# Second layer's experts with a part of the list each, their sends in the cross attention's units, their second matrices loaded beside the shared network; the values in three buffers

## The chip, the cores and the metric

The kernel runs on one core of a Trainium2 chip. The metric is the device time of one execution in microseconds (us): the median of several. Before the change it is 3898.57 us, the median of 3 runs (3896.55 to 3901.43).

Engines: PE is TensorE (matrix multiplications; PEld are its weight loads), DVE is VectorE, ACT is ScalarE, POOL is GpSimd, SP is SyncE, which here only issues DMA transfers. Everything is float32.

## The reference

A decoder of two layers on x of 32 batches x 100 tokens x 256, with a context of 361 tokens x 192 for each batch. Each layer is an attention, a cross attention and a feed-forward part, each added to x. The change touches the second layer's cross attention and its feed-forward part, a mixture of experts:

```python
def _L1_xattn_ref(x, context, ln_gamma, ln_beta, Wq, Wkv, Wo, bo, mask):
    # layer norm, queries from x, keys and values from the context,
    # 16 heads of 64, softmax over the 361 context tokens, out @ Wo + bo

def _L1_ffn_ref(x, shared_w1, shared_w2, experts_w1, experts_w2, gate_w):
    x_flat = x.reshape(T, D)                       # 3200 tokens x 256
    shared = jnp.einsum('td,dh->th', x_flat, shared_w1.T)
    shared = jnp.einsum('th,hd->td', jax.nn.silu(shared), shared_w2.T)
    gate_logits = x_flat @ gate_w.T
    top_k_gates, top_k_idx = jax.lax.top_k(gate_logits, TOP_K)     # 2 of 8 experts
    top_k_gates = jax.nn.softmax(top_k_gates, axis=1)
    gates = zeros.at[jnp.arange(T)[:, None], top_k_idx].set(top_k_gates)
    h = jnp.einsum('td,ehd->teh', x_flat, experts_w1)
    expert_out = jnp.einsum('teh,edh->ted', jax.nn.silu(h), experts_w2)
    selected = jnp.einsum('ted,te->td', expert_out, gates)
    return (shared + selected).reshape(B, S, D)

x = x + _L1_xattn_ref(_layernorm(x), ctx_768, ..., mask)
x = x + _L1_ffn_ref(_layernorm(x), ...)
```

## The kernel before

One program runs the six parts one after another: the first layer to about 1556 us of the trace, the second layer's attention to 1940, its cross attention from 1944 to 3186, the shared network of its feed-forward part from 3190 to 3414, its experts from 3418 to 3875, and a copy of the result to the end at 3898.

**The order.** In the stages of interest the instructions of PE, DVE, ACT and POOL are issued in the order of the program text (`in_order()`); in the shared network and the experts it is PE, DVE, ACT and SP that are fixed, and POOL's order is found by a scheduler. Each engine works through its queue in order, so an instruction that waits holds everything behind it. PSUM tiles for intermediate results come from a few rings: `mm` (single banks), `sc` (two tiles of two banks each), `po`.

**Cross attention** (L1404 to L1690). There are 128 units n (four for each of 32 batches); 16 units make one of 8 groups of 4 batches, and `at` is n % 16. Unit n (`turn_of`) transposes the softmax weights of unit n on PE (L1563) and multiplies them with the values (`sums`, L1581); meanwhile it makes the scores of unit n+2 (`scores`, L1531, in two halves c), the keys of unit n+3, and, for a pair of units, the values: an even unit computes context rows 0 to 255 (two chunks of 128 rows x 512 columns), an odd one the last 105 rows (two halves of 256 columns). The values pass from a PSUM tile `sc` to SBUF in two copies, one on ACT (L1517) and one on DVE (L1519), into one tile `vb`; the second half of the scores needs that `sc` tile again. `divided` computes a reciprocal on DVE (L1555), by which POOL multiplies the softmax weights of the next unit (L1556, 2.59 us); the next unit's transposes wait for this.

Between these stand, by `part_of`, the pieces of work that come once in a group: `finish` of a batch (product with Wo and the addition to x), `normed` (layer norm for the queries of the next group: at=1 the statistics on DVE, L162 to L169 with a power on POOL at L170, at=2 the centering), the queries, and `gating` of the group before: at=2 statistics, 3 centering and a store to `xn_dram`, 4 eight transposes, 5 the product with the gate's weights (eight matmuls of eight columns) and the choice of the two best experts, 6 their shares. All of it stands ahead of the unit's values, keys and `divided`.

**The list of experts.** `sorted_dram` has a row for each pair of token and expert, in blocks of 128 rows of one expert, 57 blocks at most. Its rows are first filled with `empty` (57 stores at the beginning of the cross attention; they point at a spare row). In the shared network `places_of` (two matmuls of 256 columns and a chain on DVE) computes from all choices where each pair goes: experts follow each other without a gap of more than a block. `send` writes 100 rows of a batch to their places with an indirect DMA from POOL (L1845), 64 in all. `pace` (L1891) is a copy of one element of `hT` on POOL, ahead of each eight sends, so that these are spread over the stage.

**Shared network** (L1712 to L1896). 104 units (h, m): `hidden` multiplies 256 tokens with a piece of the first matrix (L207), ACT applies Silu into `hT` (L1762, four buffers), and two units later `added` multiplies with the second matrix (L1770). SP loads tokens (`xn`, L1722), the sums so far (`acc`), and one matrix of an expert (`wx1`, 1 MB) per eight units.

**Experts** (L1900 to L1995). SP loads the experts' second matrices `wx2` (8 x 1 MB) and the blocks `xg` (four ahead, six buffers); each load of a block waits for all sends. Per block: two transposes (L1923), the first product (L207, `sc<-wx,xgT`), Silu, eight transposes, the second product, and an indirect DMA that adds the rows to `acc_dram`. The number of a block's expert is loaded into a register of PE.

Of the kernel before, what the change touches and what calls it, by code (L numbers as in the profile page):

```python
# [18 lines left out]
P = 128  # L19
B, T, D = 32, 100, 256  # L20
S2, DC = 361, 192
G = 4
# [9 lines left out]
ROW = D + E + 1  # L32
BIG = 3.0e38
# [32 lines left out]
def kernel(ctx: ExitStack, tc: tile.TileContext, io: dict, out: bass.AP):  # L66
# [1284 lines left out]
    sorted_dram = dram.tile([TILES * P, ROW], F32, name="sorted_dram")  # L1351
    wg = early.tile([P, 2, E], F32, name="f1_wg")
    nc.scalar.dma_start(wg, io["f1_wg"].rearrange("(c p) n -> p c n", p=P))
    hot = early.tile([T, 2, B, E], F32, name="hot1")
    gated = {}

    def gating(pool, g, part):
# [13 lines left out]
        elif part == 3:  # L1371
# [14 lines left out]
            for k in range(2):  # L1386
                nc.gpsimd.tensor_copy(hot[:, k, own, :], hots[:T, k])
# [4 lines left out]
            gated[g] = df, hots  # L1392
        else:
            df, hots = gated.pop(g)
# [8 lines left out]
            nc.vector.tensor_tensor(gates, gates, hots[:T, 1], ALU.add)  # L1403

    with tc.tile_pool(name="x1", bufs=2) as pool, tc.tile_pool(name="x1p", bufs=1) as fixed:
# [3 lines left out]
        def context(b):  # L1409
# [8 lines left out]
        empty = fixed.tile([P, ROW], F32, name="empty")  # L1418
        nc.gpsimd.memset(empty, 0.0)
        nc.sync.dma_start(acc_dram[NTOK:, :], empty[:, :D])  # L1420
        nc.gpsimd.iota(
            empty[:, D + E : ROW].bitcast(I32), pattern=[[0, 1]], base=NTOK, channel_multiplier=1
        )
        for t in range(TILES):
            nc.sync.dma_start(sorted_dram[t * P : (t + 1) * P, :], empty)
# [61 lines left out]
        def values(u, last, part):  # L1487
# [25 lines left out]
            for e, (at, kn, c0, n) in enumerate(parts):  # L1513
                src = ps[:kn, e, :n].rearrange("p (h d) -> p h d", d=64)
                dst = vb[:kn, 2, 4 * e : 4 * e + 4, :] if last else vb[:kn, e, :, :]
                if e == 0:
                    nc.scalar.copy(dst, src)  # L1517
                else:
                    nc.vector.tensor_copy(dst, src)  # L1519
# [53 lines left out]
        def sums(u, eT, vb, oT):  # L1573

            q4 = u % 4
            po = po_tile()
            for m in range(2):
                for k, (k0, kn) in enumerate(CCH):
                    for e in range(2):
                        h = 2 * m + e  # L1580
                        nc.tensor.matmul(  # L1581
                            po[64 * e : 64 * e + 64, m * T : (m + 1) * T],
                            vb[:kn, k, 4 * (u % 2) + h, :], eT[:kn, k, h, :],
                            start=(k == 0), stop=(k == 2), tile_position=(0, 64 * e),
                        )
            nc.vector.tensor_copy(
                oT[:, 2 * q4 : 2 * q4 + 2, :].rearrange("p m t -> p (m t)"), po[:, : 2 * T]
            )
# [17 lines left out]
        def value_tile():  # L1606
            return pool.tile([P, 3, 8, 64], F32, tag="vb", name="vb")
# [8 lines left out]
        def part_of(n):  # L1616
# [4 lines left out]
            if g + 1 < NG:  # L1621
                if at in (1, 2):
                    normed(g + 1, at - 1)
# [6 lines left out]
            if n >= 18 and (n - 18) % 16 < 5:  # L1630
                gating(pool, (n - 18) // 16, (n - 18) % 16)

        def turn_of(n):
# [10 lines left out]
            if v < NU:  # L1644
                if not last:
                    vbs[v // 2] = value_tile()
                values(v, last, 0)
            if n + 3 < NU:
                keys(n + 3, 0)
            if -1 <= n and n + 1 < NU:  # L1650
                divided(n + 1)
            if v < NU:
# [9 lines left out]
            if n >= 0:  # L1662
                if n % 4 == 0:
                    oTs[n // 4] = pool.tile([P, 8, T], F32, tag="oT", name="oT", bufs=1)
                sums(n, eT, vbs[n // 2], oTs[n // 4])

# [19 lines left out]

# [12 lines left out]
    nc.gpsimd.memset(ones8, 1.0)  # L1699

    before = fixed.tile([T, 2, P], F32, name="before")
    nc.gpsimd.memset(before, 1.0)
    nc.gpsimd.affine_select(
        before[:, 0, :], before[:, 0, :], pattern=[[1, P]], compare_op=ALU.is_gt,
        fill=0.0, base=0, channel_multiplier=-1,
    )
    pos = fixed.tile([T, 2, B], U32, name="pos1")
# [3 lines left out]
    SP = mybir.EngineType.SP  # L1711
    with tc.tile_pool(name="f1s", bufs=2, side="right") as pool, in_order(SP):  # L1712
# [73 lines left out]
        def places_of():  # L1786

            hs = pool.tile([T, B, E], F32, name="hs", bufs=1)
            nc.vector.tensor_tensor(hs, hot[:, 0], hot[:, 1], ALU.add)
            flat = hs.rearrange("p c e -> p (c e)")  # L1790
            pr = mm_tile()
            nc.tensor.matmul(pr[:, : B * E], before[:, 0, :], flat, start=True, stop=True)
            pt = mm_tile()
            nc.tensor.matmul(pt[:, : B * E], before[:, 1, :], flat, start=True, stop=True)

            tot = pool.tile([P, E, B], F32, tag="tot", name="tot", bufs=1)
            nc.vector.tensor_copy(tot, pt[:, : B * E].rearrange("p (c e) -> p e c", e=E))
            go = pool.tile([P, E, B], F32, tag="go", name="go", bufs=1)
            nc.gpsimd.memset(go, 1.0)
            nc.gpsimd.memset(go[:, :, 0:1], 0.0)  # L1800
            cum = pool.tile([P, E, B], F32, tag="cum", name="cum", bufs=1)
            nc.vector.tensor_tensor_scan(
                cum.rearrange("p e c -> p (e c)"), go.rearrange("p e c -> p (e c)"),
                tot.rearrange("p e c -> p (e c)"), 0.0, ALU.mult, ALU.add,
            )

            nb = pool.tile([P, E], F32, tag="nb", name="nb", bufs=1)
            nc.vector.tensor_scalar(
                nb, cum[:, :, B - 1], 1.0 / 128, 0.49609375, ALU.mult, ALU.add
            )  # L1810
# [4 lines left out]
            beg = pool.tile([P, E], F32, tag="beg", name="beg", bufs=1)  # L1815
            nc.vector.tensor_tensor(beg, end, nb, ALU.subtract)
            nc.vector.tensor_scalar(beg, beg, 128.0, None, ALU.mult)

            nc.vector.tensor_tensor(cum, cum, tot, ALU.subtract)
            nc.vector.tensor_tensor(cum, cum, bc(beg, 2, B), ALU.add)  # L1820
            at = pool.tile([T, B, E], F32, tag="at", name="at", bufs=1)
            nc.vector.tensor_tensor(
                at, pr[:T, : B * E].rearrange("p (c e) -> p c e", e=E),
                cum[:T].rearrange("p e c -> p c e"), ALU.add,
            )
            pf = pool.tile([T, 2, B], F32, tag="pf", name="pf", bufs=1)
            for k in range(2):
                nc.vector.tensor_tensor(hs, hot[:, k], at, ALU.mult)
                nc.vector.tensor_reduce(pf[:, k, :], hs, AX.X, ALU.add)
            nc.vector.tensor_copy(pos, pf)  # L1830
# [4 lines left out]
            nc.vector.tensor_reduce(ef, le, AX.X, ALU.add)  # L1835
            nc.vector.tensor_scalar(ef, ef, float(E - 1), None, ALU.min)
# [3 lines left out]
            )  # L1840

        def send(b):

            for k in range(2):
                put = nc.gpsimd.indirect_dma_start(  # L1845
                    sorted_dram[:, :],
                    bass.IndirectOffsetOnAxis(ap=pos[:, k, b : b + 1], axis=0),
                    xrows[b // G][:, b % G, :], None,
                )

                if sent:
                    tc.keep_in_program_order(put)
                    tc.declare_no_dep(put.ins, group="sends", reason="the places of tokens differ")
                tc.add_to_no_dep_group("sends", put.ins)
                sent.append(put.ins)

        gating(pool, NG - 1, 0)
# [7 lines left out]
        for n in range(len(units) + 2):  # L1867
# [17 lines left out]
            if n in (4, 8, 12):  # L1885
                gating(pool, NG - 1, n // 4 + 1)
            if n == 14:
                places_of()
            if n >= 27 and n % 7 == 6 and n // 7 < 3 + B // 4:

                nc.gpsimd.tensor_copy(pace, hTs[units[n]][0:1, 0:1])  # L1891
                for b in range(4 * (n // 7) - 12, 4 * (n // 7) - 8):
                    send(b)
        store(NHB - 1)
    xpool_cm.__exit__(None, None, None)
    norms_cm.__exit__(None, None, None)  # L1896
    early_cm.__exit__(None, None, None)
    wx2_cm = tc.tile_pool(name="wx2", bufs=1)
    wx2_pool = wx2_cm.__enter__()
    wx2 = wx2_pool.tile([P, E, 8, D], F32, name="wx2")  # L1900
    with tc.tile_pool(name="f1t", bufs=2, side="right") as pool, in_order(SP):
        for e in range(E):
            nc.sync.dma_start(wx2[:, e], io["f1_w2"][e + 1].rearrange("(c p) n -> p c n", p=P))
        xgs, xgTs, hgTs, experts_ = {}, {}, {}, {}

        def get(t):

            xg = pool.tile([P, ROW], F32, tag="xg", name="xg", bufs=6)
            load = nc.sync.dma_start(xg, sorted_dram[t * P : (t + 1) * P, :])
            for put in sent:  # L1910
                tc.add_manual_dep(
                    load.ins, put.name,
                    mybir.DependencyInfo(
                        mybir.DependencyClass.Sync, mybir.DependencyReason.DATA
                    ),
                    reason="all rows are there",
                )
            xgs[t] = xg
# [203 lines left out]
```

## Time and profile before

| what | value |
|---|---|
| median of 3 runs | 3898.57 us |
| the profiled execution | 3899.32 us |
| its span in the trace | 3897.6 us |
| mean granted clock of TensorE | 0.964 |
| PE busy | 3581.0 us (92%) |
| PE weight loads | 2243.9 us (58%) |
| DVE busy | 1962.1 us (50%) |
| ACT busy | 1549.4 us (40%) |
| POOL busy | 1329.7 us (34%) |

The costliest groups of the stages that the change touches (line, engine, operation, output and inputs with their shapes, count; busy us in all, mean ns of one; the engine's idle time before them and what ended most of it):

```profile
L1556 POOL TENSOR_TENSOR ex<-ex,rc 100x1444 f32<-100x1444 f32 x128 | 331.9, 2593 | 492.7 <-DVE rc L1555 492.7
L1531 PE MATMUL sc<-kT,qT 64*100 64x361 f32 x1024 | 203.1, 473 | 13.0 <-DVE vb L1519 13.0
L1563 PE MATMUL mm<-ident,ex 100*128 100x100 f32 (+1 forms) x1536 | 163.6, 256 | 8.9 <-POOL ex L1556 8.2
L207 PE MATMUL sc<-wx,xgT 128*128 x456 | 206.9, 597 | 0.3 <-DMA xg<-sorted_dram 0.3
```

Idle time of an engine costs something only where that engine is the one that the others wait for. The busy PE of the page is an average over stages with different limits, so the stages are read one by one. The chain of waits that ended last holds only the last few instructions of the program here, so the stages are read from busy sums over stretches of time, from waits within a stretch, and from the timelines of single engines. The clock of PE is the share of full speed that the chip granted it.

### The profile page before, as it was taken

What the parts mean: (1) busy time and instruction counts of PE and PEld (TensorE: products, weight loads), DVE (VectorE), ACT (ScalarE), POOL (GpSimd) and SP (SyncE); (2) the same over time, 40 slices, a digit from 0 to 9 for tenths busy, and PEclk for the clock granted to TensorE, in tenths of its full rate; (3) what the DMA queues carried; (4) which work ended last, traced back from release to release, by engine and by line L of the source; (5) the groups of instructions that cost most, each with busy time, mean ns of one, the idle gap of its engine ahead of it and who ended that gap; (6) DMA issues with size and microseconds to landing.
All of it is one profiled execution on the core that took longest, in us unless ns stands there. A gap on an engine that the chain in (4) does not pass through costs nothing. (4 is left out here: it accounts for less than half of the span.)

```text
span 3897.6 us, 65045 instructions
## 1 busy us (share of the span) xinstructions
PE 3581.0 (92%) x25566; PEld 2243.9 (58%) x25566; DVE 1962.1 (50%) x5533; ACT 1549.4 (40%) x3318; POOL 1329.7 (34%) x949
## 2 busy tenths in 40 slices
PE   7888999996889899799999999999999996999998
PEld 5665565554545453333356666666666665867675
DVE  6776666654677766565544454544544531012221
ACT  4554555553222220456644444444444441212121
POOL 3344666664444532101122232332322326012111
PEclk9999999998899989899999999999999998999999
DMA  2001000000000000400100000000000014512222
GB/s 79 2 2 58 18 20 20 18 5 15 1 1 1 1 1 0 122 1 1 34 10 16 15 20 11 20 16 15 16 15 16 15 46 140 165 35 34 34 35 57
DMA packets 94185, 110.18 MB, mean 28 GB/s; under 512 B 14142, under 2 KB 87430, under 8 KB 93290
## 3 DMA queue, kind: packets, MB, share of 16 engines
q1 hardware_dynamic: 79596, 88.40, 7.9%
q0 software_dynamic: 12304, 14.28, 2.3%
q8 instruction: 204, 3.34, 0.4%
q10 hardware_dynamic: 1982, 3.35, 0.3%
q14 instruction: 99, 0.81, 0.1%
HBM read 74.02 MB, written 35.23 MB: 28 GB/s over the span
## 5 line engine op out<-in xcount | busy, mean ns | idle before, releaser
L1556 POOL TENSOR_TENSOR ex<-ex,rc 100x1444 f32<-100x1444 f32 x128 | 331.9, 2593 | 492.7 <-DVE rc L1555 492.7
L1547 ACT ACTIVATE ex<-s,nmx 100x361 f32<-100x361 f32 x512 | 303.2, 594 | 145.4 <-DVE nmx L1538 145.4
L363 POOL TENSOR_TENSOR s<-s,nmx 100x800 f32<-100x800 f32 x128 | 194.7, 1522 | 378.1 <-DVE nmx L362 359.1
L1198 ACT ACTIVATE h<-sc,cols 128x800 f32<-128x800 f32 x256 | 222.3, 924 | 135.0 <-PE sc L1192 134.7
L207 PE MATMUL mm<-f_we,x1T 128*100 128x512 f32 x512 | 267.6, 654 | 4.3 <-DVE x L1008 2.3
L1538 DVE CUSTOM_DVE_ANT_0 s<-sc,mb 100x361 f32<-100x361 f32 x512 | 250.4, 528 | 0.1
L1519 DVE COPY vb<-sc 128x512 f32<-128x512 f32 (+1 forms) x128 | 71.5, 558 | 352.5 <-ACT vb L1517 352.5
L1974 POOL DMA_INDIRECT acc_dram<-y,xg x57 | 88.2, 1547 | 420.2 <-DVE y L1973 343.3
L1531 PE MATMUL sc<-kT,qT 64*100 64x361 f32 x1024 | 203.1, 473 | 13.0 <-DVE vb L1519 13.0
L207 PE MATMUL sc<-wx,xgT 128*128 x456 | 206.9, 597 | 0.3 <-DMA xg<-sorted_dram 0.3
L207 PE MATMUL po<-wx,hgT 128*128 x912 | 206.2, 379 | 0.3 <-ACT hgT L1956 0.3
L207 PEld LDWEIGHTS po<-wx,hgT 128*128 128x128 f32 x912 | 173.2, 190 | 47.9 <-issue 26.8
L170 POOL TENSOR_TENSOR rs<-va,neghalf 100x4 f32<-100x4 f32 (+1 forms) x96 | 92.7, 969 | 306.8 <-DVE va L169 217.8
L1973 DVE TENSOR_SCALAR y<-po,gx 128x256 f32<-128x256 f32 x57 | 27.6, 484 | 331.0 <-PE po L207 331.0
L1502 PE MATMUL sc<-x_wa,cT 128*128 128x512 f32 (+1 forms) x512 | 187.7, 489 | 0.0
L1517 ACT COPY vb<-sc 128x512 f32<-128x512 f32 (+1 forms) x128 | 61.3, 479 | 316.3 <-PE sc L1507 316.3
L1021 DVE SCALAR_TENSOR_TENSOR x<-mm,wt,x 100x256 f32<-100x256 f32 x256 | 123.6, 483 | 116.1 <-PE mm L207 109.7
L375 PE MATMUL mm<-ident,ex 100*100 100x100 f32 x1024 | 126.4, 262 | 58.9 <-ACT eT L384 22.7
L1472 PE MATMUL mm<-cT,x_wa 128*128 128x361 f32 x512 | 176.3, 467 | 0.0
L1581 PEld LDWEIGHTS po<-eT,vb 128*64 128x64 f32 (+1 forms) x3072 | 136.8, 137 | 67.3 <-issue 66.9
L1563 PE MATMUL mm<-ident,ex 100*128 100x100 f32 (+1 forms) x1536 | 163.6, 256 | 8.9 <-POOL ex L1556 8.2
L384 ACT COPY eT<-mm 100x400 f32<-100x400 f32 x192 | 92.4, 493 | 193.9 <-PE mm L375 193.4
(331 smaller groups left out, 7704.0 us busy)
## 6 DMA issues: line engine op xcount, KB each, us to landing
wx<-in_f_w SPq DMA_DIRECT2D x16, 1024.0 KB
sorted_dram<-empty SPq DMA_DIRECT2D x57, 132.5 KB
xg<-sorted_dram SPq DMA_DIRECT2D x57, 132.5 KB
cb<-in_ctx SPq DMA_DIRECT2D x32, 192.0 KB
cT<-in_ctxT SPq DMA_DIRECT2D x32, 180.5 KB
cT<-in_ctxT SPq DMA_DIRECT2D x64, 90.2 KB
x<-in_x SPq DMA_DIRECT2D x8, 400.0 KB
x_dram<-x SPq DMA_DIRECT2D x32, 100.0 KB
```

The lines of the kernel that those rows point to most:

```text
L207: nc.tensor.matmul(ps, lhsT[k], rhs[k], start=(k == 0), stop=(k == n - 1))
L363: nc.gpsimd.tensor_tensor(sm, sm, bc(nmx, 2, T), ALU.add)
L375: nc.tensor.transpose(pt[:T, j * T : (j + 1) * T], exs[s, r // 2][:, 4 * (r % 2) + j, :], ident[:T, :T],)
L1198: nc.scalar.activation(h1, both[r2][:, :, :GT], AF.Tanh, bias=col("a1_b1", o))
L1472: nc.tensor.matmul(kTs[u][c][:, :S2], x1_wa[:, m * P : (m + 1) * P], cT[:, 0, :], start=True, stop=False,)
L1502: nc.tensor.matmul(ps[:kn, e, :n], cT[:, 0, at], x1_wa[:, 1024 + c0 : 1024 + c0 + n], start=True, stop=False,)
L1531: nc.tensor.matmul(ps[:T, e, :S2], qT[p0 : p0 + 64, m, tok], kT[p0 : p0 + 64, c, :], start=True, stop=True,)
L1538: nc.vector.tensor_tensor_reduce(s[:, e, :], ps[:T, e, :S2], mb, 1.0, 3.4e38, ALU.add, ALU.min, nmx[:, e : e + 1],)
L1547: nc.scalar.activation(ex[:, 2 * c + e, :], s[:, e, :], AF.Exp, bias=nmx[:, e : e + 1], scale=-1.0, accum_out=sm[:, 2 * c + e : 2 * c + e ...
L1556: nc.gpsimd.tensor_tensor(ex, ex, bc(rc, 2, S2), ALU.mult)
L1563: nc.tensor.transpose(pt[:kn, j * T : (j + 1) * T], ex[:, j, k0 : k0 + kn], ident[:T, :T])
L1581: nc.tensor.matmul(po[64 * e : 64 * e + 64, m * T : (m + 1) * T], vb[:kn, k, 4 * (u % 2) + h, :], eT[:kn, k, h, :], start=(k == 0), stop=( ...
```

## The change

1. `sorted_dram` has a region of 3328 rows (RG) for each expert, plus 128 rows. The 57 stores of `empty` fall away. In their place, behind each expert's last row, 128 empty rows are sent (`rest`, 8 indirect DMAs), and one store fills the last 128 rows.
2. `gating` keeps a running count of each expert's rows (`base`) and has a sixth part, which gives the group's places at once: three small matmuls and a few DVE operations. `places_of` becomes `blocks_of`, which only makes the list of blocks: each block's expert and first row (`rows_at`).
3. The sends of group g (8 per group) go into units 6 to 13 after unit 16g+17, behind the unit's other work; those of the last group and the rests into units 16 to 30 of the shared network, two for each pace.
4. The norms' statistics and centerings move: `norms_of` stands behind `divided` and ahead of the end of the values (`gating` parts 0 and 1 at at=1 and 2, `normed` at at=3 and 4), and the other parts of `gating` come at at=3 to 6.
5. The values lie in three tiles (`vb0`, `vb1`, `vb2`). In odd units one copy on DVE (105x512) takes the place of two.
6. The loads of `wx2` stand in the shared network (from unit 42 on, one per six units), and the first four blocks are loaded at unit 92. Each load of a block reads its first row from `rows_at` into a register of SP.
7. At the beginning of the shared network SP first stores the spare rows of `acc_dram` and the last 128 rows of `sorted_dram`; POOL makes `empty` there.

```diff
-    sorted_dram = dram.tile([TILES * P, ROW], F32, name="sorted_dram")
+    sorted_dram = dram.tile([E * RG + P, ROW], F32, name="sorted_dram")
...
+    base = w5.tile([P, E], F32, name="base1")
+    nc.vector.tensor_scalar(base, row("iota", P), float(RG), None, ALU.mult)
...
     def gating(pool, g, part):
...
+            nc.vector.tensor_tensor(hs, hots[:T, 0], hots[:T, 1], ALU.add)
+            nc.vector.memset(hc[:, 0], 0.0)
+            for i in range(G):
+                nc.vector.tensor_tensor(hc[:, i + 1], hc[:, i], hs[:, i], ALU.add)
+            nc.vector.tensor_copy(hh, hots[:T])
...
+        else:
+            df, hots, hs, hc, hh = gated.pop(g)
+            pl = mm_tile()
+            n = G * E
+            nc.tensor.matmul(
+                pl[:, :n], before[:, 0, :], hs.rearrange("p i e -> p (i e)"),
+                start=True, stop=False,
+            )
+            nc.tensor.matmul(
+                pl[:, :n], before[:, 1, :], hc[:, :G].rearrange("p i e -> p (i e)"),
+                start=False, stop=True,
+            )
+            nc.tensor.matmul(
+                pl[:, n : n + E], before[:, 1, :], hc[:, G], start=True, stop=True
+            )
...
+            nc.vector.tensor_tensor(base, base, pl[:, n : n + E], ALU.add)
...
+            for k in range(2):
+                nc.vector.tensor_tensor(hh[:, k], hh[:, k], at, ALU.mult)
+                nc.vector.tensor_reduce(pf[:, k, :], hh[:, k], AX.X, ALU.add)
+            nc.vector.tensor_copy(pos[:, :, own], pf)
...
-        for t in range(TILES):
-            nc.sync.dma_start(sorted_dram[t * P : (t + 1) * P, :], empty)
...
-            for e, (at, kn, c0, n) in enumerate(parts):
-                src = ps[:kn, e, :n].rearrange("p (h d) -> p h d", d=64)
-                dst = vb[:kn, 2, 4 * e : 4 * e + 4, :] if last else vb[:kn, e, :, :]
-                if e == 0:
-                    nc.scalar.copy(dst, src)
-                else:
-                    nc.vector.tensor_copy(dst, src)
+            if last:
+                nc.vector.tensor_copy(vb[2][:kn].rearrange("p (e n) -> p e n", e=2), ps[:kn, :, :n])
+            else:
+                nc.scalar.copy(vb[0], ps[:, 0, :])
+                nc.vector.tensor_copy(vb[1], ps[:, 1, :])
...
         def part_of(n):
...
-                if at in (1, 2):
-                    normed(g + 1, at - 1)
...
-            if n >= 18 and (n - 18) % 16 < 5:
-                gating(pool, (n - 18) // 16, (n - 18) % 16)
+            if n >= 19 and 2 <= (n - 17) % 16 < 6:
+                gating(pool, (n - 17) // 16, (n - 17) % 16)
+
+        def norms_of(n):
+            g, at = n // 16, n % 16
+            if n >= 17 and at in (1, 2):
+                gating(pool, g - 1, at - 1)
+            if g + 1 < NG and at in (3, 4):
+                normed(g + 1, at - 3)
...
             if -1 <= n and n + 1 < NU:
                 divided(n + 1)
+            if n >= 0:
+                norms_of(n)
             if v < NU:
                 values(v, last, 1)
...
+                q, m = (n - 17) // 16, (n - 17) % 16 - 6
+                if n >= 17 and 0 <= m < 8:
+                    send(q * G + m // 2, m % 2)
...
+    def get(t):
+        xg = blocks.tile([P, ROW], F32, tag="xg", name="xg", bufs=6)
+        at = nc.sync.value_load(rows_at[0:1, t : t + 1], min_val=0, max_val=E * RG)
+        load = nc.sync.dma_start(xg, sorted_dram[bass.ds(at, P), :])
...
+        nc.sync.dma_start(acc_dram[NTOK:, :], empty[:, :D])
+        nc.sync.dma_start(sorted_dram[E * RG :, :], empty)
         gating(pool, NG - 1, 0)
         rows_of(0)
...
-            if n in (4, 8, 12):
-                gating(pool, NG - 1, n // 4 + 1)
-            if n == 14:
-                places_of()
-            if n >= 27 and n % 7 == 6 and n // 7 < 3 + B // 4:
+            if n in (4, 8, 12, 14):
+                gating(pool, NG - 1, {4: 2, 8: 3, 12: 4, 14: 5}[n])
+            if n == 18:
+                blocks_of()
+            if n >= 16 and n % 2 == 0 and n < 32:
                 nc.gpsimd.tensor_copy(pace, hTs[units[n]][0:1, 0:1])
-                for b in range(4 * (n // 7) - 12, 4 * (n // 7) - 8):
-                    send(b)
+                for k in range(2):
+                    b = B - G + (n - 16) // 2
+                    if n < 24:
+                        put(send(b, k))
+                    else:
+                        e = n - 24 + k
+                        put(nc.gpsimd.indirect_dma_start(
+                            sorted_dram[:, :],
+                            bass.IndirectOffsetOnAxis(ap=rest[:, e : e + 1], axis=0), empty, None,
+                        ))
...
+            if n >= 42 and n % 6 == 0 and n // 6 < 7 + E:
+                e = n // 6 - 7
+                nc.sync.dma_start(
+                    wx2[:, e], io["f1_w2"][e + 1].rearrange("(c p) n -> p c n", p=P)
+                )
+            if n == 92:
+                for t in range(4):
+                    get(t)
```

## The prediction

> **What bounds the kernel now.** The page's slices come first: busy tenths per 97 us and the granted TensorE clock.
>
> ```profile
> PE   7888999996889899799999999999999996999998
> PEclk9999999998899989899999999999999998999999
> ```
>
> TensorE is the wall over the second half, with one dip in both rows at slice 34, the shared network of the second layer. Next the busy sums of chosen stretches (bounds, span, then busy us of PE, weight loads, DVE, ACT, POOL, then clock, DMA share, GB/s).
>
> ```profile
> 2500.00:2700.00 200.00, 197.31 (x1379) 124.80 (x1377) 89.42 (x315) 93.30 (x259) 57.50 (x30) 1.00 0.05 15
> 3200.00:3300.00 100.00, 69.18 (x334) 60.06 (x332) 15.51 (x52) 17.14 (x40) 55.27 (x58) 0.86 0.43 133
> 3600.00:3700.00 100.00, 100.00 (x433) 71.03 (x432) 21.54 (x62) 20.35 (x25) 18.54 (x12) 1.00 0.21 34
> 3380.00:3390.00 10.00, 10.00 (x49) 8.79 (x48) 0.69 (x1) 2.19 (x6) 0.00 (x0) 1.00 1.09 354
> ```
>
> Cross attention (first row) and experts (third) run PE at 99 and 100%; the shared network (second) at 69%, with POOL busy for 55. Who holds PE there is told by the waits between 3130 and 3520 us (total, times, longest), then by PE's own timeline (start, length).
>
> ```profile
> PE sc L1770 <- ACT hT L1762: 34.3, 2, 19.7
> ACT hT L1762 <- POOL pace L1891: 42.8, 2, 23.9
> ```
>
> ```profile
> 3274.99 2.07 PE L1770 MATMUL sc<-w,hT 128*128 128x256 f32 x4 [19.68 <-ACT hT L1762]
> 3278.34 1.03 PE L1770 MATMUL sc<-w,hT 128*128 128x256 f32 x4
> 3303.50 2.07 PE L1770 MATMUL sc<-w,hT 128*128 128x256 f32 x4 [14.64 <-ACT hT L1762]
> 3308.78 1.05 PE L207 MATMUL mm<-xT,w 128*128 128x256 f32 x4
> ```
>
> POOL issues 64 sends (0.99 us, 0.30 between two) from 3228.74 on. The pace copy stands behind them and reads one of four hT buffers; ACT can't refill it, PE starves twice, and four matmuls take 2.07 us instead of 1.03 afterwards.
>
> **The change, part by part.** *Shared network.* In the changed program 8 sends and 8 rest sends stand there, two per two units, the first from the unit at which the places of the last group are ready (some 5 us for the four sends ahead of the first pace). A unit takes 1.73 us, so a pace comes 3.46 us after the last, while two sends need 2×1.29 = 2.58: POOL keeps up, and a buffer of four is read in time. Removed: 19.68 + 14.64 = 34.3 of stall, and the slow matmuls after them: 3274.99 to 3278.34 is 3.35 us for work of 1.73 (+1.6); 3303.50 to 3308.78 is 5.28 for 2.59 (+2.7). The two 256-column matmuls of places_of (0.9) go, three small ones (0.5) come. Sum −38.9. Were one pace late by a pair of sends at each of a few places, some 9 us would stay: range −30 to −39.
>
> *End of the shared network.* The loads of wx2 and of the first four blocks move ahead of its last units.
>
> ```profile
> 3189.96 1.94 PE L1735 MATMUL mm<-ident,xn 128*128 128x128 f32 x8 [4.10 <-DMA xn<-xn_dram]
> 3418.76 0.66 PE L1923 MATMUL mm<-ident,xg 128*128 128x128 f32 x2 [4.95 <-issue]
> 3421.44 5.37 PE L207 MATMUL sc<-wx,xgT 128*128 x8 [0.26 <-DMA xg<-sorted_dram]
> 3428.90 3.60 PE L207 MATMUL sc<-wx,xgT 128*128 x8
> ```
>
> PE's 4.95 us of idle (3413.8 to 3418.76) go; of the slow matmuls (5.37 against 3.60) I take 2.0 in all with the 0.66 against 0.38 before it. That is −7; but the first expert matmul then also waits for the last acc stores, which land at about 3416.7, so −6.5. Range −4 (only most of the idle) to −8.5 (with the 1.08 us between the two transposes). The eight loads of wx2 stand on SP's queue between loads of xn, acc and wx1. One stretch of eight units (13.8 us) then has about 3.1 MB to move, 224 GB/s; the fourth row of the stretches shows 354 GB/s with PE busy for all of its 10 us: 0. If they queued as long as PE waits above for one xn load (4.10) at each of two turns: +8.
>
> *Junction.* In the changed order SP issues the acc_dram tail, the last x_dram row store and the sorted_dram tail ahead of the first xn load, and the second of them waits for a POOL addition that now stands behind nine small setup operations, the zeroing of the 132.5 KB tile `empty` among them. Before, xn was issued at 3186.00 and the x_dram store at 3187.85; with two issues of 0.3 to 0.4 it comes at about 3188.7. The wait of 4.10 grows by that: +2.7 (range 2 to 5).
>
> *Cross attention.* 128 units; its waits (1970 to 3180 us), and one odd unit and the start of the next on PE and DVE:
>
> ```profile
> DVE vb L1519 <- ACT vb L1517: 348.2, 126, 6.7
> PE sc L1531 <- DVE vb L1519: 12.8, 64, 0.4
> PE mm L1563 <- POOL ex L1556: 8.2, 10, 3.2
> ```
>
> ```profile
> 3062.93 0.68 PE L1507 MATMUL sc<-x_wbv,cT 64*105 64x256 f32 x4
> 3064.66 0.77 PE L1531 MATMUL sc<-kT,qT 64*100 64x361 f32 x4
> 3062.71 0.18 DVE L1555 RECIPROCAL rc<-sm 100x4 f32<-100x4 f32 x1 [1.55 <-ACT ex L1547]
> 3064.07 0.42 DVE L1519 COPY vb<-sc 105x256 f32<-105x256 f32 x1 [1.18 <-ACT vb L1517]
> 3067.99 0.42 DVE L162 BATCH_NORM_STATS2 st<-x 100x6 f32<-100x256 f32 x1
> 3070.24 0.17 DVE L169 TENSOR_SCALAR va<-mv 100x4 f32<-100x4 f32 x1
> ```
>
> The second half of the scores (PE at 3064.66) needs the PSUM tile that DVE's copy of the values (3064.07) empties. The statistics of a norm (3067.99 to 3070.32: 2.33 us) stood ahead of the reciprocal, where they delayed only POOL's ex multiply. Now they stand behind it and ahead of that copy. At at=1 of a group: reciprocal done 3062.8, statistics to 3065.13, a copy now whole on DVE (0.69, the length of a 128x512 one) to 3065.82, scores at 3065.88 instead of 3064.66: +1.22, seven times +8.5. At at=3 the eight transposes of gating, now in that same unit, lengthen PE by 0.69 and hide that much: +0.53, seven times +3.7. At at=4 seven more small DVE operations and a centering (1.38) stand there: between 0 and 0.85 each, I take 0.25: +1.7. Waits of PE for ex that the new place avoids: 8.2 less the longest and three more at the ends of the stage that stay (3.2, 0.2, 0.6, 0.6) = −3.6. The running counts add three matmuls per group, at 0.18 (eight small ones take 1.43 at 3096.32): +3.7. Sum +14; without the collisions 0, with all at their upper ends +18.
>
> The three buffers for the values are meant to free DVE's copy from ACT's (348.2 us of waits, though PE loses only 12.8 of them). In the built program that copy still waits for ACT's, since both read one PSUM tile: 0. Were it gone, an even unit would lose its excess over an odd one (0.98 against 0.61 from keys to the second scores, 0.78 against 0.71 behind them): 64×0.45 = −29. The 64 ACT copies of 0.37 that go are no gain: ACT is busy 47%.
>
> 56 sends come onto POOL behind the ex multiply (2.59) of units at=7 to 14. POOL idles 4.49 to 6.97 ahead of the next multiply, and a send takes 1.29 with its issue: 0. If a send grew past that idle time, every microsecond beyond would cost 56. [...]
>
> *Costed at nothing.* The 57 stores of `empty` (132.5 KB each) ran at 1581 to 1619 us where SP had nothing else to do. Each block load gets a register load on SP and an address from it: a block takes some 8 us and SP does only this; the nearest row is PE's own register load, at most the 1.08 us between two transposes. Upper end +17, 0.3 per block (the 0.26 at 3421.44 that PE waits for a block's rows).
>
> **Sum.** −38.9 − 6.5 + 2.7 + 14 = −29 (−28.7). The profiled execution took 3899.3 us (span 3897.6), 0.75 above the median 3898.57: 3870.6 against the one, 3869.9 against the other. I say 3870. Its own range, from the terms' ends, is 3862 to 3879.
>
> **Rivals.**
> - *The statistics don't collide.* If DVE's and PE's slack absorbs them, cross attention stays even: 3870 − 14 = 3856. For it: the waits for ex vanish and DVE is busy under half. Against: PE is at 99%, so nothing there is slack.
> - *Part of the stall stays.* POOL's rest sends hold a pace (9, by the bound above) and the wx2 loads an xn load (8); hardly both whole, so I take 14 of the 17: 3884. For it: the same pace copy still reads hT behind sends. Against: 2.58 us of sends per 3.46.
> - *The values' wait goes after all*: 3870 − 29 = 3841. Against: the wait is in the program.
> - *The block loads become the bound* (slower). SP must read a row number into a register before each of 57 loads, in order. Two blocks' first matmuls lie 7.98 us apart (3428.90 and 3436.88); from there on the experts would follow SP, and at 9 us each they cost 57×1.02 = 58 more: 3870 + 58 = 3928. For it: nothing else on SP is so serial. Against: an issue of 0.39 and a register load of 1.08 at most make 1.5 us of work per 7.98.
> - *The change doesn't do what it says*: as to the third buffer that is already my forecast; as to the sends it would need the paces to come late, which is the second rival.
>
> **How the numbers follow.** Forecast 0.58, no collision 0.14, part of the stall 0.14, values' wait 0.04, slower rival 0.06, gains and losses that cancel 0.04. The range takes the forecast and the two neighbours with their own spread, 3853 to 3887; outside lie the last three and tails, under 0.2. What a measurement here can tell from no change is 0.2%, 7.8 us. Faster (below 3890.8): 0.58 + 0.14 + 0.04 and most of the second rival, 0.88. Within it 0.05; slower 0.07.
>
> **What would show it.** Shared network: no wait of PE for hT, its stretch some 39 us shorter, clock 1.0. End: PE busy through the last units into the first transposes. Cross attention: PE waits for DVE's vb at at=1 and 3 of each group, about 1.2 and 0.5 us, while its other units keep their lengths; the copy of vb1 still ends its wait on ACT. Experts: a block at 7.9. Wrong if the sends on POOL stretch past 5 us in cross attention, if PE waits for xn or acc in the middle of the shared network, or if a block grows.

## The result and the profile after

The changed kernel takes 3896.56 us (median of 14 runs, 3891.25 to 3902.78), the kernel before beside it 3896.48 (14 runs): a ratio of 0.9998, interval 0.999 to 1.0006. Nothing is gained and nothing lost; 3870 had been forecast. The profiled execution of the changed kernel has a span of 3893.1 us, that of before 3897.6.

PE's timeline, cut at the first instruction of each stage, says where the forecast 29 us went (all in us):

| stretch | before | after | difference | forecast |
|---|---|---|---|---|
| start to the first weight transposes of the cross attention | 1973.1 | 1970.8 | −2.3 | 0 |
| from there to those of its last unit | 1205.1 | 1246.3 | **+41.2** | +14 |
| to the first token transposes (junction) | 11.8 | 16.2 | +4.5 | +2.7 |
| to the first block transposes (shared network, its end) | 228.8 | 183.8 | **−45.0** | −45.4 with the next row |
| to the end of the span | 478.8 | 476.0 | −2.9 | |

The page's slices of the changed kernel, and the busy sums of a stretch of the cross attention, of the shared network and of the experts (columns as before):

```profile
PE   7888999996889899799999999999999998999998
...
PEclk9999999998899999899999999999999999999999
```

```profile
2500.00:2700.00 200.00, 193.09 (x1365) 123.04 (x1365) 101.21 (x336) 86.41 (x240) 67.56 (x38) 0.99 0.07 20
3240.00:3340.00 100.00, 100.00 (x493) 88.29 (x492) 17.86 (x70) 25.59 (x61) 17.99 (x24) 1.00 0.49 165
3600.00:3700.00 100.00, 100.00 (x425) 69.59 (x424) 22.25 (x65) 19.89 (x26) 20.22 (x13) 1.00 0.22 34
```

The dip at slice 34 is gone: in the shared network PE is busy for 100 of 100 us at full clock, where it was 69 of 100. But in the same stretch of the cross attention it is busy for 193.1 of 200 us instead of 197.3, at a clock of 0.99. PE's waits there (1970 to 3180; total, times, longest), and the largest from 3130 to 3520:

```profile
PE sc L1575 <- DVE vb L1563: 30.1, 61, 2.4
PE sc L1575 <- DVE vb L1560: 15.2, 14, 1.5
PE mm L1607 <- POOL ex L1600: 0.6, 1, 0.6
```

```profile
PE mm L1812 <- DMA xn<-xn_dram: 8.6, 1, 8.6
PE mm L1607 <- POOL ex L1600: 3.5, 1, 3.5
PE mm L2009 <- issue: 1.0, 1, 1.0
```

The scores' wait for DVE's copies of the values grew from 12.8 to 45.3 us (30.1 + 15.2); the waits for POOL's multiply fell to 0.6; no wait for hT is left, and the wait for the first tokens doubled from 4.1 to 8.6. The worst wait for a copy, 2.40, stands in the unit at=4 of a group (DVE, POOL and PE timelines, start and length):

```profile
2168.30 0.17 DVE L1599 RECIPROCAL rc<-sm 100x4 f32<-100x4 f32 x1
2168.39 3.64 DVE L177 TENSOR_SCALAR xn<-x,mv,rs 100x256 f32<-100x256 f32 x4
2171.96 0.67 DVE L1563 COPY vb<-sc 128x512 f32<-128x512 f32 x1
```

```profile
2168.65 2.59 POOL L1600 TENSOR_TENSOR ex<-ex,rc 100x1444 f32<-100x1444 f32 x1 [3.58 <-DVE rc L1599]
```

```profile
2172.69 1.08 PE L1575 MATMUL sc<-kT,qT 64*100 64x361 f32 x4 [2.40 <-DVE vb L1563]
2173.70 2.27 PE L1625 MATMUL po<-eT,vb 128*64 128x100 f32 x24
```

Four centerings took 3.64 us. The row that the forecast used had four in 1.38, and POOL's next multiply came only behind them (kernel before, DVE and POOL):

```profile
3076.66 1.38 DVE L176 TENSOR_SCALAR x<-x,mv,rs 100x256 f32<-100x256 f32 x4
```

```profile
3078.58 2.59 POOL L1556 TENSOR_TENSOR ex<-ex,rc 100x1444 f32<-100x1444 f32 x1 [4.49 <-DVE rc L1555]
```

In the changed kernel POOL's multiply runs from 2168.65 to 2171.24, and the DVE group ends 0.8 behind it. The next view gives the instructions of one line in the cross attention (count, shortest/median/longest in ns, first and last start). In the trace 14 of the 56 take 2.68 to 2.70, one of each group of four:

```profile
L177 DVE TENSOR_SCALAR xn<-x,mv,rs x28: 379/402/2700, 2009.0 to 2975.1; 100x256 f32<-100x256 f32 x28
L177 DVE TENSOR_SCALAR x<-x,mv,rs x28: 399/402/2689, 2143.9 to 3110.1; 100x256 f32<-100x256 f32 x28
```

The one that starts while the multiply is on waits for its end: 2.70 is 2.59 and a tenth. The statistics' `BATCH_NORM_STATS2`, in the same place beside the same multiply, runs on:

```profile
L163 DVE BATCH_NORM_STATS2 st<-x x57: 393/394/408, 1998.2 to 3127.5; 100x6 f32<-100x256 f32 x57
```

So do the copies out of PSUM (0.69 beside the multiply or apart from it). After the 2.40 the 24 matmuls of the sums took 2.27 instead of 1.26, at a granted clock of 0.50 (2174 to 2176).

### The profile page after: what moved, and what is told of

Same layout as the page of the kernel before. It is cut to its first block, busy times and chain, and to the rows that moved or that the text cites. A ratio compares the mean times of both kernels' runs of the same rounds, so it can differ in the third digit from the quotient of the medians.

```text
span 3893.1 us, 65394 instructions
## 1 busy us (share of the span) xinstructions
PE 3583.1 (92%) x25610; PEld 2250.5 (58%) x25610; DVE 2034.2 (52%) x5647; ACT 1523.8 (39%) x3254; POOL 1338.3 (34%) x941
## 5 line engine op out<-in xcount | busy, mean ns | idle before, releaser
L1614 ACT COPY eT<-mm 128x400 f32<-128x400 f32 (+1 forms) x256 | 125.9, 492 | 105.6 <-PE mm L1607 105.5
L1625 PE MATMUL po<-eT,vb 128*64 128x100 f32 (+1 forms) x3072 | 165.9, 258 | 0.0
```

The costliest lines, as they stand in the source:

```text
L1625: nc.tensor.matmul(po[64 * e : 64 * e + 64, m * T : (m + 1) * T], vb[k][:kn, 256 * (u % 2) + 64 * h : 256 * (u % 2) + 64 * h + 64], eT[:kn ...
```

## The experiments

Lengths of one unit by its place `at` in a group (start of its weight transposes to those of the next unit, median over the six full groups, the second to the seventh), and of all units together, from PE's timelines. At at=7 to 15 the kernels whose copies aren't taken apart differ from before by less than 0.1.

| kernel | at=0 | 1 | 2 | 3 | 4 | 5 | 6 | all |
|---|---|---|---|---|---|---|---|---|
| before | 12.27 | 7.58 | 8.85 | 6.91 | 12.98 | 8.49 | 9.53 | 1205.1 |
| changed | 12.21 | 8.63 | 9.37 | 8.59 | 17.24 | 6.91 | 10.20 | 1246.3 |
| e1 norms ahead | 12.21 | 7.60 | 8.67 | 8.41 | 13.84 | 6.91 | 10.20 | 1213.7 |
| e2 move alone | 12.27 | 8.36 | 9.37 | 8.32 | 14.90 | 6.91 | 9.54 | 1226.3 |
| e3 centerings ahead | 12.22 | 8.63 | 8.67 | 8.58 | 13.84 | 6.91 | 10.21 | 1223.0 |
| e4 copies apart | 11.77 | 8.63 | 9.46 | 8.58 | 16.36 | 6.91 | 9.76 | 1225.8 |
| e5 strided result | 12.21 | 8.63 | 9.37 | 8.59 | 16.67 | 6.91 | 10.42 | 1247.6 |
| e10 with accumulator | 12.21 | 8.63 | 8.67 | 8.58 | 14.17 | 6.91 | 10.21 | 1225.4 |
| e11 centerings on ACT | 12.21 | 8.63 | 12.33 | 9.33 | 19.84 | 7.13 | 10.21 | 1295.3 |
| e12 all three | 11.77 | 7.60 | 8.23 | 8.42 | 13.84 | 6.91 | 9.76 | 1188.3 |

Three profiles with the same cross attention (the changed kernel, e9 and e6) have 1246.3, 1246.5 and 1247.5 in all, so these lengths carry the verdicts; single times of one kernel scatter by 5 us and more to either side. At at=4 the changed kernel takes 15.91 in two of the six groups and 17.14 to 17.45 in the other four; e4 and e5 vary there in the same way, so their medians at at=4 say little. Each ratio below is to the kernel before that ran beside it.

**e1, the norms ahead of the reciprocal again.**

```diff
+            if n >= 0:
+                norms_of(n)
             if -1 <= n and n + 1 < NU:
                 divided(n + 1)
-            if n >= 0:
-                norms_of(n)
```

> The changed kernel with the norms' statistics and centerings put ahead of the reciprocal again; sends, regions, three value tiles and the moved loads stay. Theory (the place of the norms costs the cross attention 41 us, of which 6.5 per group are seen at at=1 to 6; the 36 us of the shared network's end and stalls are real): a group gets back to about 0.5 above the one of before, the time falls by 35 to 37, to about 3860. Rival (the sends on POOL, the running counts or the value tiles cost it): the time stays above 3885 and the units at=7 to 14 or the odd units are longer than before.

3864.28 us, ratio 0.9922 (0.99 to 0.9945). The cross attention loses 32.6 of its 41.2, and the shared network's gain comes out. The sends, the value tiles and the counts are all still there, so they aren't the cause. Of a group 1.2 stays, not 0.5: 0.67 at at=6 (the counts' matmuls) and 0.57 behind at=3, where PE waits for POOL's multiply, since the statistics are ahead of its reciprocal again. Such waits are 8.9 us in all here.

**e2, the move alone on the kernel before.**

```diff
-                if at in (1, 2):
-                    normed(g + 1, at - 1)
...
-            if n >= 18 and (n - 18) % 16 < 5:
-                gating(pool, (n - 18) // 16, (n - 18) % 16)
+            if n >= 19 and 2 <= (n - 17) % 16 < 5:
+                gating(pool, (n - 17) // 16, (n - 17) % 16)
+
+        def norms_of(n):
+            g, at = n // 16, n % 16
+            if n >= 17 and at in (1, 2):
+                gating(pool, g - 1, at - 1)
+            if g + 1 < NG and at in (3, 4):
+                normed(g + 1, at - 3)
...
                 divided(n + 1)
+            if n >= 0:
+                norms_of(n)
```

> The kernel before with nothing but the norms moved behind the reciprocal (and the gating one unit earlier, as in the change). Theory: cross attention longer by 37 (41 less the three matmuls of the running counts and the junction's share), time about 3933. Rival (the cost comes from sends or counts, not from the place): within 8 us of 3896.5.

3916.31, ratio 1.0045 (1.003 to 1.0061), cross attention +21.2 instead of 37: the theory's direction and half its size. What is missing against the changed kernel stands in the table: 0.27 each at at=1 and 3 (the third value tile's copy takes 0.69 on DVE alone, not 0.42), 2.3 at at=4 (the seven small DVE operations of the counts, about 1 us in the timeline, stand ahead of the reciprocal there, and the wait of 2.40 instead of 1.4 is followed by slow matmuls in four of the six groups), 0.67 at at=6 (the counts' matmuls). The move and the added work make each other dearer.

**e3, the centerings alone ahead of the reciprocal** (`norms_of` takes the part, 0 for statistics, 1 for centerings).

```diff
+            if n >= 0:
+                norms_of(n, 1)
             if -1 <= n and n + 1 < NU:
                 divided(n + 1)
             if n >= 0:
-                norms_of(n)
+                norms_of(n, 0)
```

> The changed kernel with the centerings alone ahead of the reciprocal; the statistics stay behind it. Theory A (a DVE centering that runs beside POOL's multiply is held until the multiply is over, one in four takes 2.7 us instead of 0.4, and this is the larger part): units at=2 and at=4 to 6 lose 0.5 and some 3.3 a group, time about 3870; the centerings are back at 0.41 us each, the statistics still cost 1.0 at at=1 and 1.0 at at=3. Theory B (order on DVE alone, four centerings of 0.41 ahead of the values' copy): no more than 1.4 a group comes back, time about 3887 or above.

3872.48, ratio 0.9936 (0.9916 to 0.9955): theory A. 23.3 of the 41.2 were the centerings; the statistics, by the step from e3 to e1, 9.3.

**e5, the result of one centering with a step.**

```diff
-                xn = pool.tile([T, G, D], F32, tag="xn", name="xn", bufs=1)
+                xn = pool.tile([T, G, D, 2], F32, tag="xn", name="xn", bufs=1)[:, :, :, 0]
```

> The changed kernel with one centering of the two (that of the query norm, at=4) writing its result with a step of two elements; place, count and inputs are the same. [...] Rival (the wait is for a buffer or for POOL's result, whatever the form): one in four still takes 2.7 us, time within 5 of the changed kernel.

Forecast, if the contiguous result is the condition: none of this centering's four at 2.7, time 3876 to 3884. A miss: 3899.42, and the longest centering of the query norm is as long as it was.

```profile
L177 DVE TENSOR_SCALAR xn<-x,mv,rs x28: 382/402/2705, 2004.9 to 2970.1; 100x256 f32<-100x256 f32 x28
```

The shortest and the median didn't change either: that the elements of the result lie side by side isn't the condition. The ratio of 0.9957 says little. The kernel before that ran beside e5 to e8 took 3916.56 us, beside all others 3896.46 to 3899.23, while e5 and e6 took what the changed kernel takes elsewhere. Why the kernel before alone was slower there isn't settled; e5 to e8 are compared with the changed kernel by medians and stretches.

**e10, the same instruction in the form that also writes an accumulator.** The values that this form wrote are not those of the plain one, and why stays open; so only its times are used.

```diff
+    def centered_too(dst, src, n, mv_rs, np_=T):
+        mv, rs = mv_rs
+        too = small.tile([P, G], F32, tag="too", name="too")
+        for i in range(n):
+            nc.vector.tensor_scalar(
+                dst[:, i, :], src[:, i, :], mv[:np_, i, 0:1], rs[:np_, i : i + 1],
+                ALU.subtract, ALU.mult, accum_out=too[:np_, i : i + 1],
+            )
```

> The changed kernel with both centerings in the form of the same DVE instruction that also writes out a sum; place, count, inputs and outputs are the same. [...] Rival (anything of SBUF that DVE touches there is held until the multiply ends): one in four still takes 2.7, time within 5 of the changed kernel.

Forecast, if the form is the condition: no centering over 0.7, at=4 at 14.5 or less, time 3872 to 3882. It took 3877.76, ratio 0.9954 (0.9939 to 0.997). In the same place, beside the same multiply, no centering is held (the same view of this kernel):

```profile
L186 DVE TENSOR_SCALAR_CACHE_REDUCE xn<-x,mv,rs x28: 506/534/539, 2011.1 to 2956.8; 100x256 f32<-100x256 f32 x28
...
L186 DVE TENSOR_SCALAR_CACHE_REDUCE x<-x,mv,rs x28: 533/537/541, 2146.0 to 3090.1; 100x256 f32<-100x256 f32 x28
```

Each is a third longer than a plain one (0.53 against 0.40), and the cross attention is 21.0 shorter. The units that hold no centering kept their lengths to 0.02. So 21 of the 41 us come from the hold of one plain form beside POOL's multiply, with the slow matmuls that followed it.

**e11, both centerings on ACT.**

```diff
+    def centered_on_act(dst, src, n, mv_rs, np_=T):
+        mv, rs = mv_rs
+        nb = small.tile([P, G], F32, tag="nb", name="nb")
+        nc.gpsimd.tensor_scalar(nb[:np_, :n], mv[:np_, :n, 0], -1.0, None, ALU.mult)
+        nc.gpsimd.tensor_tensor(nb[:np_, :n], nb[:np_, :n], rs[:np_, :n], ALU.mult)
+        for i in range(n):
+            nc.scalar.activation(
+                dst[:, i, :], src[:, i, :], AF.Identity,
+                bias=nb[:np_, i : i + 1], scale=rs[:np_, i : i + 1],
+            )
```

> The changed kernel with both centerings on ACT (with the product of mean and scale on POOL behind the scale), at the same place of the program. [...]

Forecast, if the multiply doesn't hold ACT: 0.4 to 0.5 for a centering, none over 0.7, at=4 at 15 or less, time 3870 to 3882; if it does, over 1 for a centering. It took 3946.21, ratio 1.0133 (1.0118 to 1.0149). ACT's centerings take 0.58 to 0.60 each, none longer, but the time was forecast badly: the small product `nb` stands behind the multiply on POOL's queue (in one unit the multiply ends at 2150.49 and `nb` starts there), ACT waits for it, and the copy of vb0 stands behind it on ACT. Since ACT ran only once the multiply was over, this doesn't show whether ACT would have been held.

**e4, the copies of the values apart.**

```diff
-                nc.scalar.copy(vb[0], ps[:, 0, :])
-                nc.vector.tensor_copy(vb[1], ps[:, 1, :])
+                one = nc.scalar.copy(vb[0], ps[:, 0, :])
+                two = nc.vector.tensor_copy(vb[1], ps[:, 1, :])
+                tc.add_to_no_dep_group(f"v{u}", one.ins)
+                tc.declare_no_dep(two.ins, group=f"v{u}", reason="both only read")
```

> The changed kernel with DVE's copy of vb1 no longer waiting for ACT's copy of vb0 (both only read the PSUM tile and write different tiles; the scores wait for both). If that wait makes the even units longer than the odd ones: 0.37 to 0.45 less in each of 64 even units, 24 to 29 in all, time about 3870, no wait of 0.20 ahead of the scores. Rival (PE then waits for ACT's copy, or for something behind, as long): within 5 us of the changed kernel.

3874.23, ratio 0.9943 (0.9924 to 0.9962). Even units lose 0.44 to 0.45 (12.21 to 11.77 at at=0), as the forecast had it for a wait that goes, except at=2, where the held centering stands ahead of DVE's copy, and at=4. In all 20.6. So the third buffer alone did next to nothing (12.27 to 12.21 at at=0), and the wait that it was for is worth 0.45 in an even unit.

**e6, the first tokens' load ahead of the two stores.**

```diff
+        rows_of(0)
         nc.sync.dma_start(acc_dram[NTOK:, :], empty[:, :D])
         nc.sync.dma_start(sorted_dram[E * RG :, :], empty)
         gating(pool, NG - 1, 0)
-        rows_of(0)
```

> The changed kernel with the first load of tokens ahead of the two stores of empty rows on SP's queue. Theory (the wait of 8.6 for xn at the junction is made of an issue 2.5 late and a landing 2 us longer behind the stores): the wait falls to about 4, the time by 4 to 5. Rival (it waits for memory that the cross attention gives up late): wait stays above 7.

The wait falls from 8.57 to 4.03; the median, 3895.92, can't show it. From the beginning of this wait to the second run of first-matrix products it is 15.5 in the changed kernel and 12.4 here, so 3.1 of the 4.5 is kept, and 1.4 is given back at once: PE waits 0.94 for DVE's copy of the turned tokens, and the next 12 matmuls take 4.81 instead of 4.28.

**e7, e8, e12: what goes together.** e7 has e1's and e4's edits, e12 e6's as well. e8 has e4's and e6's, and the norms and the gating in the units of the kernel before, with the counts at at=7 and the sends from at=8.

> Norms ahead of the reciprocal and the copies apart together. If the two costs are independent: 3864 less 0.45 for each of 64 even units = 3835. If the shorter even units leave POOL's multiply too little time (rival), PE's waits for ex grow from 12.5 to 25 or more and the time stays above 3845.

> The changed kernel with the norms and the gating in the units that the kernel before gave them (running counts at at=7, sends from at=8 on), the copies apart, and the tokens' load first. Sum: cross attention 1205 of before, plus 0.67 for each of 7 groups (three matmuls), less 0.45 for 64 even units = 1181 against 1246, and 4.5 at the junction: 3896.5 - 65 - 4.5 = 3827. Rival (the sends one unit later come into units that end a group, or POOL's multiply gets the bound): above 3840.

> Norms ahead of the reciprocal, copies apart and the tokens' load first, the rest as changed. Sum from the runs so far: 41.2 - 8.6 = 32.6 in the cross attention for the first, 28.8 - 2 for the second (even units that no norm holds), 4.5 for the third: 64 below the changed kernel, about 3833 where that takes 3896.5; not over 3836.

3838.53 (e7), 3836.04 (e8) and 3837.93 (e12, ratio 0.9852, 0.9837 to 0.9867). The cross attentions are 1189.4, 1189.0 and 1188.3, some 57 below the changed kernel's: the two parts add up (32.6 + 20.6 = 53.2, and 4 more where no held centering is in the way of the copy). All three are 58 to 60 us, 1.5%, below the 3896.5 that both kernels take in the first comparison, and don't differ clearly from each other; each stayed 3 to 9 above its sum. e8's units are 8 longer than its sum: at=5 takes 9.07, with the counts' DVE operations ahead of the reciprocal, and at=2 keeps its 8.85, the norms standing ahead of the copies. e12's profile has the wait for the tokens at 4.0 against 8.7 in e7's, but its median doesn't show it.

**e9, the changed kernel once more.**

> The changed kernel itself once more, beside the kernel before and the following three, since the ratios of the last four runs were taken where the kernel before took 3916.56 us instead of 3896 to 3899 while kernels like the changed one took 3896 to 3899. If the kernel before is the one that differs between chips: ratio 0.995 to 0.9955 where it takes about 3916, 0.9998 where it takes about 3897. If the changed kernel moves along: 0.9998 in both.

3896.40 against 3896.46, ratio 0.9997 (0.9988 to 1.0006): no change, a second time. Of the slower kernel before beside e5 to e8 it tells nothing, since here that took 3896.

## Why the prediction was wrong

**What bounds the kernel**: right. PE bounds the cross attention (busy for 197.3 of 200 us before), so what lengthens a unit there is paid in full.

**Shared network and its end**: right, −45.0 and 2.9 more behind it against −45.4 (the first expert matmuls take 3.67 instead of 5.37). Of eight pace copies three waited for their hT, and nothing waited for a pace.

**Junction**: mechanism right, +4.5 against +2.7. The xn load was issued 2.5 us after PE had ended, as forecast, instead of 0.1; that it would also land 2 us later (6.1 after its issue against 4.0) wasn't in the sum, though inside the range of 2 to 5.

**Cross attention**: the step that failed, +41.2 against +14. By its terms:

- The waits for POOL's multiply went, as forecast (8.2 to 0.6 in that view).
- The statistics behind the reciprocal were put at 8.5 + 3.7, less 3.6 for the waits for POOL that go: 8.6. Their place costs 9.3, such waits counted in, by e3 against e1. Near. (The rest of the 41.2, 8.6, is what e1 leaves; its waits for POOL are in that, so the split holds for this order of the runs.)
- The running counts' matmuls: 0.67 a group at at=6 against 0.54. Right.
- The sends cost nothing: at=7 to 14 kept their lengths, at 1.02 us a send (median; the longest of the 64 took 1.54).
- The centerings, the term that failed. "At at=4 seven more small DVE operations and a centering (1.38) stand there: between 0 and 0.85 each, I take 0.25: +1.7", and of the one at at=2 the sum said nothing. They cost 23.3 (e3), of which 21.0 go with the form that is held (e10): four took 3.64, not 1.38. The 1.38 came from a place where POOL was idle; the move took the instruction to where POOL's multiply always runs.

The row that shows this was in the trace of before, in the first layer, where the same line of the same helper runs beside a 2.46 us addition on POOL (one group of four, the addition, and the line's shortest, median and longest):

```profile
1113.03 3.42 DVE L176 TENSOR_SCALAR yo<-x,mv,rs 100x256 f32<-100x256 f32 x4
```

```profile
1113.19 2.46 POOL L944 TENSOR_TENSOR xl<-xl,rows 100x1024 f32<-100x1024 f32 x1
```

```profile
L176 DVE TENSOR_SCALAR yo<-x,mv,rs x32: 400/407/2458, 1113.0 to 1563.5; 100x256 f32<-100x256 f32 x32
```

Four in 3.42 instead of 1.38, and a longest of 2458 against a median of 407, say what the rows of the cross attention itself could not.

The forecast had no term for what an instruction on POOL does to one on DVE. The runs show its size: beside a multiply of 2.59 the plain form takes 2.70 and the form that writes out its accumulator at most 0.54 (e10). By what mechanism the one is held and the other not, no run shows.

**Rivals.** "The statistics don't collide" and "part of the stall stays" were wrong, and the values' wait stayed, as forecast; its price of 0.45 an even unit is borne out by e4, but not for all 64 of them (−29): e4 gained 20.6, and e7 24.3 over e1, since at=4 gained nothing there. The block loads never became a bound (PE 100 of 100 us in the experts). The outcome, gains and losses that cancel, had been given a chance of 0.04 and no mechanism.

**Its sums.** The stretches of the shared network add up to −39.0, not −38.9, which changes nothing. The ends of all terms, added up, give 3853 to 3887, which is the outer range; they don't give the "own range" of 3862 to 3879.

## What to carry to other kernels

When an instruction is moved, its duration has to be taken from a row where the same engines run beside it, not from its old place: look at the longest instance of its line, not at the mean. A plain SBUF-to-SBUF `tensor_scalar` on DVE beside a long POOL operation lasted here until that was over (2.70 beside a multiply of 2.59, 0.40 apart from it); it belongs ahead of what releases POOL (e1, e3), or in a form that isn't held (e10 shows the time of one, at most 0.54, though not one with the right values). And a buffer buys nothing as long as the built program keeps the wait (12.27 to 12.21 at at=0): read the waits, not the tiles.

## What the runs showed of the hardware

The hold is on whole instructions: of four centerings the first, begun before the multiply, took 0.38, the second 2.70, the last two 0.40 each. A step of two in the result doesn't lift it (2.705 at the longest, e5), the form that writes an accumulator does (0.541 at the longest, e10). In four of six groups of the changed kernel the stall of 2.40 on PE was followed by slow matmuls (24 in 2.00 to 2.27 instead of 1.26; granted clock 0.50 from 2333.7 to 2337), in two, after the same 2.40, it was not (1.26; clock 1.00 from 2494.7 to 2498). No stall of 1.47 (at=1) or of 1.4 (at=4 of e2) was. So a held instruction on DVE can cost PE more than the wait that the view shows, and the same wait does not always cost the same.
